# Attention weights read by VectorE and ScalarE from a lasting PSUM bank instead of an SBUF copy, in a graph attention layer

## The chip, the cores and the metric

The kernel runs on one core of one Trainium2 chip. The metric is the device time of one execution in microseconds. The engines are called PE (TensorE, whose weight loads are PEld), DVE (VectorE), ACT (ScalarE), POOL (GpSimd) and SP (SyncE, which here issues transfers).

## The reference

There are 12500 nodes with 256 features and 200000 edges sorted by their destination. A layer norm and a ReLU give h; then one graph attention layer with 8 heads of 32 features is computed, with gelu, a second layer norm, and residuals. Cut to what matters:

```python
h = relu(layernorm(x))
q, k, v = (h @ Wq + bq), (h @ Wk + bk), (h @ Wv + bv)      # each [n, 8, 32]
logits = einsum('ehd,ehd->eh', q[dst], k[src]) / sqrt(32)
seg_max = segment_max(logits, dst)
expv = exp(logits - seg_max[dst])
agg = segment_sum((expv / segment_sum(expv, dst)[dst])[:, :, None] * v[src], dst)
out = agg.reshape(n, 256) + (h @ Wskip + bskip)
y = h + gelu(out)
result = x + layernorm(y) * gamma + beta
```

## The kernel before, in words

First `project` normalizes x and writes a table of h and a table of k and v to HBM; beside it a plan is made of where each edge stands. This takes about the first 300 us. The rest is `walk_streams`.

The sorted edges are cut into 8 streams (S) of 25000 edges, which are walked side by side in 66 steps (NST). A step takes 384 slots (CH) of each stream, as 3 tiles (K) of 128 edges; the last step has 2 tiles, so that there are 197 tiles in all. Slot 0 of a step carries the running sums of the node that was open at the end of the step before. For tile j of step c:

- `gather` (L1047): 8 indirect transfers, issued by POOL, fetch the rows of k and v of 128 edges of each stream into one of 6 SBUF buffers `kv`. The gathers for step c + 2 are issued after the weighing that frees a buffer.
- `spread` (L1085, PE): matmuls with a one-hot matrix `to_e` spread the queries `qw` of the step's nodes over the edges, half of the streams at a time, into one of two PSUM buffers `ps_qe`. The queries themselves are projected in the walk (`turn_windows` L1023, `queries` L1036 and L1040, copied by ACT at L1026 and L1042); the one-hot matrices come from `hot_e` (L1062, L1064) and `hot_n` (L1073, L1075).
- `times` (L1094, DVE): product of queries and keys, a half at a time. `total` (L1101, DVE): sum over the 32 features, into L.
- `turn` (L1111, PE): transposes L into the PSUM bank `ps_x`, partitions 0 to 63 (8 streams by 8 heads), columns of tile j. For tile 0 ACT also copies the running maximum into column 0 (L1113).

Once per step, when all three tiles are turned:

- `maxima` (L1122, L1123, L1125, DVE): a scan forward (its result goes to the upper half of the bank), a scan backward, and the difference W. `exponent` (L1129, ACT).
- `turn_back` (L1137, PE): three transposes put the weights back, edges on partitions, into the first 192 columns of the bank; `weights` (L1145, ACT) copies them to SBUF as `w`, 128 x 192.
- `carried` (L1151, L1153, ACT): copies the carried denominators, and the weights of tiles 1 and 2 as the first 8 columns of `vw`. `weigh` (L1160, DVE): for each tile, `vw` is v times the weights; tile 0 has a second multiply for the denominators (L1165).
- `add_up` (L1184, PE) sums `vw` over the edges of each node in three groups of streams; ACT copies the sums (L1196) and the open node's row into the next step's tile 0 (L1202); SP stores them.

Beside that, in most steps from the tenth on, a `Pair` of blocks of finished nodes is normalized and stored (fetch, transposes L845, skip product L862, gelu L871, DVE statistics L874 to L880, root L884, factors L888 and L889, normal L894, shift L901 and L904, scale L908 and L910).

What sets the order: `keep` ties every instruction to the one before it on the same engine, so each engine runs the list in the order in which the loop from L1272 writes it. The loop at step c goes: halves of tile 2 of step c, `total`, `turn`; weighing of tile 2 of step c - 1; `maxima`; additions of step c - 1 around `exponent` and `turn_back`; `weights`; `carried`; tile 0 of step c + 1; weighing of tile 0; `hot_n`; `turn` of tile 0 of step c + 1; the pair's work and the projection for step c + 2; tile 1 of step c + 1, its `turn`; weighing of tile 1; additions of tiles 0 and 1; statistics of the pair. The framework adds the semaphore waits that the tiles' reads and writes call for.

In the kernel before, the bank is a tile that is taken anew for each step from a pool of one buffer (L1110), and its last readers are the scans and the copy L1145.

Of the kernel before, what the change touches and what calls it, by code (L numbers as in the profile page):

```python
# [28 lines left out]
F32 = mybir.dt.float32  # L29
# [10 lines left out]
P = 128  # L40
HEADS = 8
# [4 lines left out]
S = 8  # L46
K = 3
CH = K * P
# [705 lines left out]
def walk_streams(tc, N, HID, NST, KL, many, ident, idx, d0_row, slot_row, near, near_n, e_tab, pen_tab, h_tab,  # L754
# [6 lines left out]
    nc = tc.nc  # L761
# [3 lines left out]
    SH = S * HEADS  # L765
# [6 lines left out]
    def keep(ins):  # L772

        before = latest.get(ins.ins.engine)
        if before is not None:
            tc.add_manual_dep(ins.ins, before, mybir.DependencyInfo(
                mybir.DependencyClass.NoSync, mybir.DependencyReason.DATA), reason="kept order")
        latest[ins.ins.engine] = ins.ins.name
        return ins
# [168 lines left out]
    with ExitStack() as es:  # L948
# [8 lines left out]
        work = pool_of("work", 2)  # L957
# [3 lines left out]
        xt_ps = pool_of("xt_ps", 1, space=PSUM)  # L961
# [22 lines left out]
        def tiles_of(c):  # L984
            return KL if c == NST - 1 else K


        step = [dict() for _ in range(NST + 3)]

        def where(s):  # L990
# [115 lines left out]
        def turn(c, j):  # L1106

            g = step[c]
            if j == 0:
                g["xt"] = xt_ps.tile([P, 512], F32, name="ps_x")  # L1110
            keep(nc.tensor.transpose(g["xt"][:SH, j * P:(j + 1) * P], g["L"][:, j, :], ident))  # L1111
            if j == 0:
                keep(nc.scalar.copy(g["xt"][:SH, 0:1],  # L1113
                                    low0 if c == 0 else step[c - 1]["M"][:, CH - 1:]))

        def maxima(c):
            g = step[c]
            n = tiles_of(c) * P
            X, R, pen = g["xt"][:SH, :n], g["xt"][SH:, :n], g["pen"]
            M = g["M"] = work.tile([SH, CH], F32, name="M")[:, :n]  # L1120
            W = g["W"] = work.tile([SH, CH], F32, name="W", bufs=1)[:, :n]
            keep(nc.vector.tensor_tensor_scan(R, pen[:SH, :n], X, -BIG, op0=OP.add, op1=OP.max))  # L1122
            keep(nc.vector.tensor_tensor_scan(mirrored(M, 0, n), mirrored(pen[SH:, :], 1, n),  # L1123
                                              mirrored(R, 0, n), -BIG, op0=OP.add, op1=OP.max))
            keep(nc.vector.tensor_tensor(W, X, M, op=OP.subtract))  # L1125

        def exponent(c):
            W = step[c]["W"]
            keep(nc.scalar.activation(W, W, AF.Exp))  # L1129

        def turn_back(c):
            g = step[c]

            n = tiles_of(c)
            ps = g["xt"][:, :K * SH].rearrange("p (k n) -> p k n", k=K)
            for j in range(n):
                keep(nc.tensor.transpose(ps[:, j, :], g["W"][:, j * P:(j + 1) * P],  # L1137
                                         ident[:SH, :SH]))

        def weights(c):  # L1140
            g = step[c]
            n = tiles_of(c)
            ps = g["xt"][:, :K * SH].rearrange("p (k n) -> p k n", k=K)
            g["w"] = work.tile([P, K, SH], F32, name="w", bufs=1)
            keep(nc.scalar.copy(g["w"][:, :n, :], ps[:, :n, :]))  # L1145

        def carried(c):

            g = step[c]
            g["vw"] = [work.tile([P, S, SUMS], F32, name="vw", bufs=K) for _ in range(K)]  # L1150
            keep(nc.scalar.copy(wden[c % 2][0:1], g["kv"][0][0:1, :, HID - HEADS:HID]))  # L1151
            for j in range(1, tiles_of(c)):
                keep(nc.scalar.copy(g["vw"][j][:, :, :HEADS],  # L1153
                                    g["w"][:, j, :].rearrange("p (s h) -> p s h", s=S)))

        def weigh(c, j):
            g = step[c]
            t = g["vw"][j]
            wj = g["w"][:, j, :].rearrange("p (s h) -> p s h", s=S)
            keep(nc.vector.tensor_tensor(  # L1160
                t[:, :, HEADS:].rearrange("p s (h d) -> p s h d", h=HEADS),
                wj[:, :, :, None].to_broadcast([P, S, HEADS, D]),
                g["kv"][j][:, :, HID:].rearrange("p s (h d) -> p s h d", h=HEADS), op=OP.mult))
            if j == 0:
                keep(nc.vector.tensor_tensor(t[:, :, :HEADS], wj, wden[c % 2], op=OP.mult))  # L1165
# [106 lines left out]
        for c in range(NST - 1):  # L1272

            pair_next = None
            if c in due:
                pair_next = Pair(fin, due[c][0],
                                 lambda: hot_ps.tile([P, 2, KC, P], F32, name="ps_hot"),
                                 lambda: ag_ps.tile([P, 2 * HID], F32, name="ps_a").rearrange(
                                     "p (b d) -> p b d", b=2),
                                 keep)  # L1280
            if c + 3 < NST:
                windows(c + 3)
            for half in range(2):
                times(c, K - 1, half)
                spread(c + 1, 0, half)
            total(c, K - 1)
            turn(c, K - 1)
            if c:
                weigh(c - 1, K - 1)
                gather_next(c - 1, K - 1)  # L1290
            maxima(c)
            if before:
                before.factors()
            if c:
                add_up(c - 1, 0, range(K - 1, K))
                add_up_products(c - 1, 1)
            exponent(c)
            turn_back(c)
            if c:
                add_up_results(c - 1, 1)  # L1300
            weights(c)
            if c:
                add_up(c - 1, 2)
            carried(c)
            for half in range(2):
                times(c + 1, 0, half)
                spread(c + 1, 1, half)
            total(c + 1, 0)
            weigh(c, 0)
            gather_next(c, 0)  # L1310
            for j in range(K):
                hot_n(c, j)
            turn(c + 1, 0)
            if before:
                before.normal()
                before.shifted()
            if pair:
                pair.turn()
                pair.divisors()
                pair.divide()  # L1320
                pair.skip()
            if before:
                before.scale()
                before.store(0)
                before.store(1)
            if pair_next:
                pair_next.fetch()
            if c == NST - 2:
                for i in range(4):
                    last(i)  # L1330
            if c + 2 < NST:
                turn_windows(c + 2, 0)
                queries(c + 2, 0)
                hot_e(c + 2, 0)
            if pair:
                pair.add()
                table_of(AF.Gelu)
                pair.gelu()
            if c + 2 < NST:
                turn_windows(c + 2, 1)  # L1340
                queries(c + 2, 1)
            for half in range(2):
                times(c + 1, 1, half)
                if tiles_of(c + 1) == K:
                    spread(c + 1, K - 1, half)
            total(c + 1, 1)
            turn(c + 1, 1)
            weigh(c, 1)
            gather_next(c, 1)
            if c + 2 < NST:  # L1350
                for i in range(1, S // 2):
                    hot_e(c + 2, i)
            add_up(c, 0, range(K - 1))
            if c + 2 < NST:
                penalties(c + 2)
            if c + 3 < NST:
                prefetch(c + 3)
            if c == NST - 2:
                weigh(c, K - 1)
                add_up(c, 0, range(K - 1, K))  # L1360
                add_up(c, 1)
                if pair_next:
                    pair_next.turn()
                    pair_next.skip()
            if pair:
                table_of(AF.Sqrt)
                pair.stats()
                pair.root()
                table_of(AF.Exp)
            if c == NST - 2:  # L1370
                add_up(c, 2)
            before, pair = pair, pair_next
            if c > 1:
                step[c - 2] = None

        c = NST - 1
# [14 lines left out]
        if before:  # L1391
            before.factors()
        turn_back(c)
        weights(c)
        carried(c)
        weigh(c, 0)
        if pair:
# [53 lines left out]
        if extra:  # L1451
            with tc.If(many > 0):
                for m in extra:
                    p = Pair(fin, m, lambda: hot_ps.tile([P, 2, KC, P], F32, name="ps_hot"),
                             lambda: ag_ps.tile([P, 2 * HID], F32, name="ps_a").rearrange(
                                 "p (b d) -> p b d", b=2), lambda ins: ins)
# [349 lines left out]
```

## Time and profile before

| what | value |
| --- | --- |
| time, median of 7 runs | 3083.33 us (3051.05 to 3121.55) |
| the profiled execution's own time | 3099.2 us |
| its span, first to last instruction | 3097.4 us |
| granted TensorE clock, mean | 0.797 |
| the copy to SBUF (L1145) | 66 of 317 ns, 20.9 us in all |
| the copies into `vw` (L1153) | 131 of 238 ns, 25.2 us in all |
| the weighings (L1160) | 197 of 2286 ns, 450.2 us in all; 288.5 us idle before them |
| the transposes of L (L1111) | 197, 65.0 us in all |
| the scans forward (L1122) | 66 of 957 ns; 221.4 us idle before them |

A group's row gives the busy time, the mean of one instruction, and the idle time of its engine just before it with what ended that. In a timeline each row has its start, its duration, engine, line, operation, output and inputs, the count of merged instructions, and in brackets the idle time before it with what ended it. A matmul's end is modelled: its row says when it was issued, and the start of the instruction that waited for it says when it was done. An idle time put down to "remote" or "issue" has no releaser that the profile could name.

### The profile page before, as it was taken

Reading aid. Unit: us, or ns where it says so; the run is one execution under the profiler, and the core shown is the slowest. Engines: PE = TensorE matmul, PEld = TensorE weight load, DVE = VectorE, ACT = ScalarE, POOL = GpSimd, SP = SyncE. Lnnn points to the kernel's source line nnn. Section 1 sums busy time; section 2 is a strip of 40 time slices with the busy share of each in tenths; the row PEclk is TensorE's granted clock in tenths of the full one; section 3 lists DMA queues with packets and bytes.
Section 4 is the critical chain, followed back from the end, with each engine's and each line's share of the span. In section 5 each row is a group of like instructions: output and inputs, shape, how many; then the busy total and the mean of one; then the engine's idle time right before and its main releaser. Section 6 shows DMA issues by size and latency. Waiting matters only on the chain. (4 is left out here: it accounts for less than half of the span.)

```text
span 3097.4 us, 33801 instructions
## 1 busy us (share of the span) xinstructions
PE 2018.4 (65%) x10196; PEld 1161.5 (37%) x10196; DVE 1942.0 (63%) x2207; ACT 1111.0 (36%) x2583; POOL 1714.1 (55%) x1648
## 2 busy tenths in 40 slices
PE   7893666566566566577576667576666666665666
PEld 3441433333333343344343344343334333333333
DVE  8782665665566566566566566566566665666674
ACT  4330222222333344343344333343343343343343
POOL 2205476777566565556665566654656655655550
PEclk9996776877788788777787787777787878787786
DMA  8767466667576666666665676665666756765652
GB/s 277 259 221 233 129 193 190 197 186 216 171 212 193 196 185 187 188 195 198 212 200 171 189 211 194 199 187 165 207 193 192 210 173 183 207 194 175 194 157 80
DMA packets 285958, 597.79 MB, mean 193 GB/s; under 512 B 52295, under 2 KB 178452, under 8 KB 283584
## 3 DMA queue, kind: packets, MB, share of 16 engines
q0 software_dynamic: 128768, 423.23, 46.2%
q1 hardware_dynamic: 156466, 171.81, 17.4%
q8 instruction: 84, 1.38, 0.2%
q14 instruction: 110, 0.90, 0.1%
q10 hardware_dynamic: 530, 0.47, 0.1%
HBM read 512.83 MB, written 82.47 MB: 192 GB/s over the span
## 5 line engine op out<-in xcount | busy, mean ns | idle before, releaser
L1047 POOL DMA_INDIRECT kv<-kv_tab,idx x1576 | 1672.9, 1061 | 1085.9 <-issue 492.7
L1094 DVE TENSOR_TENSOR kv<-ps_qe,kv 128x1024 f32<-128x1024 f32 x394 | 468.2, 1219 | 402.3 <-remote 183.7
L1160 DVE TENSOR_TENSOR vw<-w,kv 128x2048 f32<-128x2048 f32 x197 | 450.2, 2286 | 288.5 <-ACT kv L1202 241.9
L1085 PE MATMUL ps_qe<-qw,to_e 64*128 64x256 f32 x3152 | 471.5, 440 | 19.0 <-issue 17.2
L1101 DVE TENSOR_REDUCE L<-kv 128x64 f32<-128x2048 f32 x197 | 450.4, 2286 | 6.7
L1085 PEld LDWEIGHTS ps_qe<-qw,to_e 64*128 64x128 f32 x3152 | 338.0, 218 | 169.1 <-issue 118.2
L1040 PE MATMUL ps_hot<-w_q,hwT 128*128 128x256 f32 x792 | 256.6, 470 | 121.0 <-issue 56.2
L1184 PE MATMUL ps_a<-vw,to_n 128*32 128x264 f32 (+1 forms) x2344 | 295.6, 494 | 43.6 <-DVE vw L1160 25.0
L1196 ACT COPY sums_w<-ps_a 128x264 f32<-128x264 f32 x130 | 49.3, 379 | 641.7 <-remote 412.6
L1064 ACT ACTIVATE to_e<-ps_hot,ones 128x384 f32<-128x384 f32 x264 | 145.6, 580 | 346.3 <-remote 256.0
L1184 PEld LDWEIGHTS ps_a<-vw,to_n 128*32 128x32 f32 (+1 forms) x2344 | 108.5, 141 | 396.6 <-issue 337.9
L1040 PEld LDWEIGHTS ps_hot<-w_q,hwT 128*128 128x128 f32 x792 | 170.0, 230 | 191.5 <-issue 77.3
L1062 PE MATMUL ps_hot<-et,near 48*128 48x384 bf16 x264 | 83.8, 357 | 239.3 <-ACT to_e L1064 148.6
L1073 PE MATMUL ps_hot<-near_n,et 48*128 48x384 bf16 x197 | 61.8, 357 | 272.5 <-ACT to_n L1075 161.6
L1137 PE MATMUL ps_x<-ident,W 64*128 64x64 f32 x197 | 31.0, 276 | 273.3 <-ACT W L1129 206.2
L248 PE MATMUL ps_kv<-w_kv,hT 128*128 128x512 f32 x392 | 188.7, 625 | 24.9 <-ACT hT L141 20.9
L1122 DVE TENSOR_TENSOR_SCAN ps_x<-pen,ps_x 64x384 f32<-64x384 f32 x66 | 63.1, 957 | 221.4 <-remote 137.8
L982 ACT ACT_TABLE_LOAD x138 | 177.1, 1283 | 2.4
L1042 ACT COPY qw<-ps_hot 128x256 f32<-128x256 f32 (+1 forms) x132 | 63.2, 479 | 280.4 <-PE ps_hot L1040 138.8
L1111 PEld LDWEIGHTS ps_x<-ident,L 128*64 128x64 f32 x197 | 22.5, 114 | 355.4 <-issue 282.1
L862 PE MATMUL ps_a<-w_s,hT 128*128 128x256 f32 x368 | 139.3, 544 | 16.3 <-ACT hT L848 11.4
L1202 ACT COPY kv<-ps_a 1x264 f32<-1x264 f32 x388 | 142.9, 368 | 6.3
(283 smaller groups left out, 2350.8 us busy)
## 6 DMA issues: line engine op xcount, KB each, us to landing
kv<-kv_tab,idx POOLq DMA_INDIRECT x1576
kv_tab<-kvo SPq DMA_DIRECT2D x14, 1536.0 KB
hw<-h_tab SPq DMA_DIRECT2D x264, 64.0 KB
table<-sums_w SPq DMA_DIRECT2D x264, 61.9 KB
pen<-pen_tab SPq DMA_DIRECT2D x66, 192.5 KB
sums<-table SPq DMA_DIRECT2D x92, 132.0 KB
x_f<-in_x_dram SPq DMA_DIRECT2D x92, 128.0 KB
h<-h_tab SPq DMA_DIRECT2D x92, 128.0 KB
```

Source lines behind the costliest of these rows:

```text
L248: ins = nc.tensor.matmul(ps_kv, hT[:, c, :], w_kv[:, c, :], start=c == 0, stop=c == KC - 1)
L862: self.keep(nc.tensor.matmul(self.ps[:, b, :], self.hT[:, b, c, :], w_s[:, c, :], start=False, stop=False, skip_group_check=True))
L982: keep(nc.scalar.activation(dummy[:, 1:2], dummy[:, 0:1], function))
L1040: keep(nc.tensor.matmul(ps[:, b, :], g["hwT"][:, b, k, :], w_q[:, k, :], start=False, stop=k == KC - 1, skip_group_check=True))
L1047: nc.gpsimd.indirect_dma_start(out=t[:, s, :], out_offset=None, in_=kv_tab[:, :], in_offset=bass.IndirectOffsetOnAxis(ap=idx[:, s, j, c:c ...
L1064: keep(nc.scalar.activation(step[c]["to_e"][:, i, :], ps[:, :CH], AF.Relu, scale=-1.0, bias=ones))
L1085: keep(nc.tensor.matmul(ps[:, b, a, :], g["to_e"][r, 2 * half + a, j * P:(j + 1) * P], g["qw"][r, (half + a) * half, :], start=True, stop= ...
L1094: keep(nc.vector.tensor_tensor(k, g["qe", half].rearrange("p b a d -> p a b d"), k, op=OP.mult))
L1101: keep(nc.vector.tensor_reduce(g["L"][:, j, :].rearrange("p (s h) -> p s h", s=S), g["kv"][j][:, :, :HID].rearrange("p s (h d) -> p s h d" ...
L1160: keep(nc.vector.tensor_tensor(t[:, :, HEADS:].rearrange("p s (h d) -> p s h d", h=HEADS), wj[:, :, :, None].to_broadcast([P, S, HEADS, D] ...
L1184: keep(nc.tensor.matmul(ps[at:at + w, :], g["to_n"][:, j, i * P + at:i * P + at + w], g["vw"][j][:, s, :], start=j == 0, stop=j == tiles_o ...
L1202: keep(nc.scalar.copy(step[c + 1]["kv"][0][0:1, s, HID - HEADS:], ps[at:at + 1, :]))
```

## The change

The bank becomes one tile for the whole walk, `turned`, with 512 columns. Columns 0 to 383 hold the transposed L of the step, as before. `turn_back` now writes the weights of tile 0 to columns 0 to 63, those of tile 1 to columns 384 to 447 and those of tile 2 to columns 448 to 511. `weights` and its copy L1145 are removed: `carried` and `weigh` read the weights in the bank. The order in which the loop writes the rest of a step is the same. (The queries are projected in the walk in both kernels.)

```diff
+        turned = xt_ps.tile([P, CH + 2 * SH], F32, name="ps_x")
...
         def turn(c, j):
             g = step[c]
+            keep(nc.tensor.transpose(turned[:SH, j * P:(j + 1) * P], g["L"][:, j, :], ident))
             if j == 0:
-                g["xt"] = xt_ps.tile([P, 512], F32, name="ps_x")
-            keep(nc.tensor.transpose(g["xt"][:SH, j * P:(j + 1) * P], g["L"][:, j, :], ident))
-            if j == 0:
-                keep(nc.scalar.copy(g["xt"][:SH, 0:1],
+                keep(nc.scalar.copy(turned[:SH, 0:1],
                                     low0 if c == 0 else step[c - 1]["M"][:, CH - 1:]))
...
-            X, R, pen = g["xt"][:SH, :n], g["xt"][SH:, :n], g["pen"]
+            X, R, pen = turned[:SH, :n], turned[SH:, :n], g["pen"]
...
+        def weight(j):
+            at = CH + (j - 1) * SH if j else 0
+            return turned[:, at:at + SH].rearrange("p (s h) -> p s h", s=S)
+
         def turn_back(c):
-            g = step[c]
-            n = tiles_of(c)
-            ps = g["xt"][:, :K * SH].rearrange("p (k n) -> p k n", k=K)
-            for j in range(n):
-                keep(nc.tensor.transpose(ps[:, j, :], g["W"][:, j * P:(j + 1) * P],
-                                         ident[:SH, :SH]))
-
-        def weights(c):
-            g = step[c]
-            n = tiles_of(c)
-            ps = g["xt"][:, :K * SH].rearrange("p (k n) -> p k n", k=K)
-            g["w"] = work.tile([P, K, SH], F32, name="w", bufs=1)
-            keep(nc.scalar.copy(g["w"][:, :n, :], ps[:, :n, :]))
+            for j in range(tiles_of(c)):
+                keep(nc.tensor.transpose(weight(j).rearrange("p s h -> p (s h)"),
+                                         step[c]["W"][:, j * P:(j + 1) * P], ident[:SH, :SH]))
...
             for j in range(1, tiles_of(c)):
-                keep(nc.scalar.copy(g["vw"][j][:, :, :HEADS],
-                                    g["w"][:, j, :].rearrange("p (s h) -> p s h", s=S)))
+                keep(nc.scalar.copy(g["vw"][j][:, :, :HEADS], weight(j)))
...
-            wj = g["w"][:, j, :].rearrange("p (s h) -> p s h", s=S)
+            wj = weight(j)
...
             turn_back(c)
             if c:
                 add_up_results(c - 1, 1)
-            weights(c)
```

More of the change, by code (lines that the diff above doesn't have):

```diff
@@ L1393, in walk_streams @@
         turn_back(c)
-        weights(c)
         carried(c)
```

## The prediction

> **What bounds the kernel now.** I read the page first (spans and engines), then the groups of the touched lines, then VectorE's waits, and last the timeline of one step of the walk, instruction by instruction.
>
> ```profile
> span 3097.4 us, 33801 instructions
> PE 2018.4 (65%) x10196; PEld 1161.5 (37%) x10196; DVE 1942.0 (63%) x2207; ACT 1111.0 (36%) x2583; POOL 1714.1 (55%) x1648
> ```
>
> No engine is full. The 66 steps are bound by the hand-written order: each engine runs its list, and a step lasts as long as the hand-overs between PE, DVE and ACT. Between the reductions L1101 of tile 2 in steps 1 and 63 a step takes 41.86 us on average. So a copy's busy time says little; what counts is who waits for it.
>
> ```profile
> L1153 ACT COPY vw<-w 128x64 f32<-128x64 f32 x131 | 25.2, 238 | 0.0
> L1145 ACT COPY w<-ps_x 128x192 f32<-128x192 f32 x66 | 20.9, 317 | 12.3 <-issue 5.2 <-PE ps_hot L1073 3.4 <-PE ps_x L1137 1.3
> ```
>
> The removed copy is 20.9 us of an engine that is 64% idle.
>
> ```profile
> DVE vw L1160 <- ACT kv L1202: 241.9, 48, 18.0
> DVE kv L1094 <- remote: 149.6, 42, 8.5
> ```
>
> The first weighing waits for the row copies L1202 (the sums carried over from the step before), not for the weights.
>
> ```profile
> 2070.95 0.76 ACT L1202 COPY kv<-ps_a 1x264 f32<-1x264 f32 x2
> 2071.74 2.29 DVE L1160 TENSOR_TENSOR vw<-w,kv 128x2048 f32<-128x2048 f32 x1 [4.31 <-ACT kv L1202]
> 2071.89 0.39 ACT L1153 COPY vw<-w 128x64 f32<-128x64 f32 x2
> ...
> 2073.33 0.42 PE L1111 MATMUL ps_x<-ident,L 128*64 128x128 f32 x1
> ...
> 2073.95 0.22 DVE L1165 TENSOR_TENSOR vw<-w,wden 128x64 f32<-128x64 f32 x1
> ...
> 2079.31 2.29 DVE L1101 TENSOR_REDUCE L<-kv 128x64 f32<-128x2048 f32 x1
> ...
> 2081.52 2.28 DVE L1160 TENSOR_TENSOR vw<-w,kv 128x2048 f32<-128x2048 f32 x1
> ...
> 2086.79 0.69 DVE L874 TENSOR_TENSOR sums<-sums,h 128x512 f32<-128x512 f32 x1 [2.99 <-ACT sums L871]
> ...
> 2088.19 0.30 DVE L880 BATCH_NORM_AGGREGATE mv<-st 128x2 f32<-128x6 f32 x2
> ...
> 2091.13 0.30 PE L1111 MATMUL ps_x<-ident,L 128*64 128x128 f32 x1
> ...
> 2093.53 1.23 DVE L1094 TENSOR_TENSOR kv<-ps_qe,kv 128x1024 f32<-128x1024 f32 x1 [5.03 <-DMA kv<-kv_tab,idx]
> 2098.03 1.23 DVE L1094 TENSOR_TENSOR kv<-ps_qe,kv 128x1024 f32<-128x1024 f32 x1 [3.28 <-remote]
> 2098.10 1.72 ACT L1064 ACTIVATE to_e<-ps_hot,ones 128x384 f32<-128x384 f32 x3 [8.21 <-remote]
> ...
> 2099.29 2.29 DVE L1101 TENSOR_REDUCE L<-kv 128x64 f32<-128x2048 f32 x1
> ...
> 2101.49 2.28 DVE L1160 TENSOR_TENSOR vw<-w,kv 128x2048 f32<-128x2048 f32 x1
> ...
> 2104.18 0.30 PE L1111 MATMUL ps_x<-ident,L 128*64 128x128 f32 x1
> ...
> 2104.52 0.96 DVE L1122 TENSOR_TENSOR_SCAN ps_x<-pen,ps_x 64x384 f32<-64x384 f32 x1 [0.74 <-PE ps_x L1111]
> ```
>
> See where the weighing of tile 1 stands (2081.52): ten microseconds before PE issues the transpose of the next step's tile 1 (2091.13). It fills a stretch in which VectorE would be idle. Then both VectorE (2098.03) and ScalarE (2098.10) start together, long after PE's modelled ends (2091.4): PE finished the spreading matmuls and the transpose late, at about 2098. I call that moment T2: the later of the modelled end of the transpose and, where the two halves of L1094 stand over 1.3 us apart, the start of the second half. Over steps 1 to 62 PE's lateness at T2 averages 2.9 us.
>
> **The change, part by part.** The columns in the shared bank are disjoint, but the built program of the changed kernel adds waits all the same. Followed by their counts: the weighing of tile 0 waits for both L1153 copies; the transpose of the next tile 0 waits for L1165; the weighings of tiles 1 and 2 wait for the transposes of the next step's tile 1 and the same step's tile 2, written just ahead of them. Before, VectorE took these weighings with no wait for PE.
>
> [...]
>
> *Removed copy.* 66 of 317 ns, ending at 2064.43 in the quoted step; ScalarE's next copy starts at 2070.67, held by PE. Worth 0; at most −20.9 us.
>
> *Weights read from PSUM.* Two L1094 (one operand in PSUM, 1024 each) take 2 x 1219 = 2438 ns, one L1160 (none in PSUM, 2048) 2286: the difference of 152 ns is one fixed start. Taken as 0; upper end 197 x 0.152 = 30 us; lower end 0, as the fixed part cannot be less than the one paid. The L1153 copies: L1145's short form from PSUM (128 wide) takes 238 ns like L1153's own: 0.
>
> *Tile 0.* Its weighing starts when the copies end, 2071.89 + 0.39 = 2072.28 instead of 2071.74: 0.54 later. L1165 then ends at 2074.17 + 0.54, and the transpose that stood at 2073.33 starts about 2074.8: 1.5 us later. Behind it on PE lie the shift matmuls, the skip product, both projections and the spreading, a chain with ScalarE that ends at T2. Where PE was already late it costs nothing: in the same way for steps 1 to 62 it is 0.92 us on average, 57 us.
>
> *Tile 1.* Its weighing moves from 2081.52 to T2, 16.5 us; in all 62 steps T2 is later than it (by 1.9 us at least, 11.2 on average). What is late next is VectorE: behind it are the statistics (0.69 + 0.75 + 0.30 with gaps: 1.7, in the 43 of 62 steps that hold a pair) and both halves of L1094. Before, the second half started at T2; now it starts at T2 + 2.3 + 1.7 + 1.2 (first half) = 5.2 later, without a pair 3.5. Where T2 was not late, the first half already overlapped; averages 5.1 and 3.3. 43 x 5.1 + 19 x 3.3 = 281 us. Eight gathers of L1047 are issued after this weighing; with them landing some 16 us later, cover is the median 23.8 us from the last issue to use. Gone, it would cost its shortfall. PE's add-up of tile 1 waits too, 0.8 us, ahead of spreading that waits for VectorE anyway. SP's transfers are not moved.
>
> *Tile 2.* Its weighing (2101.49) waits for the transpose, and the scan for the weighing. Before: scan 2.94 us after the reduction ended (2101.58). Now the spreading runs during the reduction, since VectorE is the late one; transpose 0.45, weighing 2.29: 2.74. Against each step's own scan the median is −0.9 us, 62 x −0.9 = −56: taken, as the middle step. Ends: if all PE lateness there vanishes, mean −2.9 (−177); if all stays, the weighing comes on top, +2.28 (+141).
>
> Sum: 0 + 0 + 57 + 281 − 56 = +282 us on the profiled execution's 3099.2 (span 3097.4), 3381; that execution stood 15.9 above the median, so **3365 us**. With the lower ends: −21 + 57 + 281 − 177 = +140, 3223; with the upper: 30 + 57 + 281 + 141 = +509, 3592.
>
> **The rivals.**
> 1. *Not slower.* VectorE's delay gives PE rest and its lateness vanishes at both places: T2 62 x −2.9 = −181 and the scan −177: −21 + 281 + 57 − 181 − 177 = −41, 3042. It decides once the lateness falls by 338 of these 358 us. For it: the clock is granted at 0.78 to 0.80 through the walk. Against: step 23 took 57.4 us, and the halves of the next step's L1094 still stood 5.2 apart.
> 2. *Worse.* PE gets slower as it idles more. PE is busy 1731.7 us from 300 to 3000; were the granted clock 0.75 instead of 0.797 and all of that on the path, 6%: 108 us more, 3473, or with the upper ends 3700. For: the clock is below full now, with PE idle 35% of the time. Against: the same idle gaps are there now. [...]
> 3. *The new waits do not bind* because they are met early, or only addresses count: then only tile 0 costs, +57: 3140. Against: T2 is later in every step.
>
> **How the numbers follow.** Forecast 0.82; rival 1 0.04; rival 2 beyond the range 0.09; rival 3 0.05. The range 3210 to 3530 holds the forecast's ends short of the last, and leaves out the rivals. About 1% (31 us) is what a measurement of this kernel can tell from no change: faster 0.02, same 0.03 (rival 1 splits), slower 0.95.
>
> **What would show it.** Right: L1145 gone; the weighing's group gaining idle time released by PE's transposes of L, some 11 us per step on tile 1; the transposes' wait released by L1165; the reductions of tile 2 some 46 us apart instead of 41.9; the weighing's mean still near 2286 ns. Wrong: a weighing of tile 1 still ahead of the transpose, a mean above 2.4 us, a granted clock much off 0.80, or gathers that VectorE waits for.

## The result, and the profile after

The changed kernel takes 3365.62 us (median of 18 runs, 3357.10 to 3374.93) against 3084.30 us for the kernel before (46 runs, 3046.99 to 3125.02): a ratio of 1.0945, 95% interval 1.0923 to 1.0968, or +281 us. The forecast was 3365 us. The total came out as forecast; the places where the time went did not, and most of what follows is about that.

In the changed kernel the lines have moved a little: the weighing is L1153 (L1160 before), the copies of the weights into their rows L1147 (L1153), the copies of the sums L1189 and L1195 (L1196 and L1202), the products of VectorE L1096 (L1094), the reduction L1103 (L1101). The lines of the page and of its groups that answer to those shown of before:

```profile
span 3366.3 us, 33800 instructions
PE 2274.3 (68%) x10196; PEld 1255.0 (37%) x10196; DVE 1944.5 (58%) x2207; ACT 1097.8 (33%) x2517; POOL 1551.5 (46%) x1648
...
L1153 DVE TENSOR_TENSOR vw<-ps_x,kv 128x2048 f32<-128x2048 f32 x197 | 451.3, 2291 | 1187.2 <-ACT vw L1147 595.0
```

VectorE and ScalarE do the same work as before. The copy L1145 is gone (66 instructions fewer on ScalarE). A weighing that reads PSUM takes 2291 ns instead of 2286. But the idle time just before the weighings is 1187.2 us. The waits of the engines name who ends it (total, times, longest):

```profile
DVE vw L1153 <- ACT vw L1147: 595.0, 64, 11.5
DVE vw L1153 <- PE ps_x L1111: 532.1, 67, 12.5
```

The first line is tile 0, which waits for the copies of the other tiles' weights; the second is tile 1, which waits for the transpose of the next step. Now one step in order of time (start, duration, engine, line; the brackets hold the idle time ahead and who ended it):

```profile
2199.13 0.96 DVE L1122 TENSOR_TENSOR_SCAN ps_x<-pen,ps_x 64x384 f32<-64x384 f32 x1
...
2200.19 2.91 PE L1177 MATMUL ps_hot<-vw,to_n 128*64 128x264 f32 x12
...
2200.33 0.38 ACT L1189 COPY sums_w<-ps_a 128x264 f32<-128x264 f32 x1 [7.22 <-PE ps_a L1177]
...
2203.03 0.58 PE L1138 MATMUL ps_x<-ident,W 64*128 64x64 f32 x3
...
2212.66 0.38 ACT L1189 COPY sums_w<-ps_hot 128x264 f32<-128x264 f32 x1 [10.09 <-remote]
...
2215.04 0.33 ACT L1147 COPY vw<-ps_x 128x64 f32<-128x64 f32 x2
...
2215.40 2.29 DVE L1153 TENSOR_TENSOR vw<-ps_x,kv 128x2048 f32<-128x2048 f32 x1 [8.78 <-ACT vw L1147]
...
2217.88 0.42 PE L1111 MATMUL ps_x<-ident,L 128*64 128x128 f32 x1 [1.50 <-DVE vw L1158]
...
2234.32 0.30 PE L1111 MATMUL ps_x<-ident,L 128*64 128x128 f32 x1
...
2234.66 2.29 DVE L1153 TENSOR_TENSOR vw<-ps_x,kv 128x2048 f32<-128x2048 f32 x1 [8.51 <-PE ps_x L1111]
2236.86 0.68 DVE L874 TENSOR_TENSOR sums<-sums,h 128x512 f32<-128x512 f32 x1
...
2238.55 2.36 DVE L1096 TENSOR_TENSOR kv<-ps_qe,kv 128x1024 f32<-128x1024 f32 x2
...
2243.61 2.29 DVE L1153 TENSOR_TENSOR vw<-ps_x,kv 128x2048 f32<-128x2048 f32 x1 [0.39 <-issue]
2245.94 0.96 DVE L1122 TENSOR_TENSOR_SCAN ps_x<-pen,ps_x 64x384 f32<-64x384 f32 x1
```

Every wait that the forecast named is there: the transpose that waits for L1158 (1.50), the weighing of tile 1 behind the transpose (8.51), then the statistics and both halves of L1096, now back to back ("x2"), then the weighing of tile 2 ahead of the scan. What the forecast did not have is the wait of 10.09 us at 2212.66: PE issued the products of ps_hot at 2200.19, their modelled end is 2203.10, and ScalarE's copy gets them 9.6 us later. Everything down to the first weighing at 2215.40 stands behind this copy.

I cut each step into stretches by the instructions' times and averaged them over steps 1 to 62, as in the forecast. The last column counts the instructions of ScalarE and VectorE between 400 and 2950 us that wait for PE and start over 1 us after the modelled end of what they wait for (and after their own engine's last instruction), with the sum of these delays; where two engines wait for one delay it counts twice. In the changed kernels the first weighings are counted as well, since they read the bank, though what they wait for are ScalarE's copies.

| kernel | reduction of tile 2 to scan | scan to first weighing | to tile 1's first product | to tile 2's second product | step | late, sum us |
|---|---|---|---|---|---|---|
| before | 7.88 | 11.84 | 4.79 | 16.09 | 41.86 | 206, 1036 |
| changed | 5.27 | 16.74 | 5.05 | 17.78 | 46.08 | 118, 1079 |
| difference | −2.61 | +4.90 | +0.26 | +1.69 | +4.22 | |

(The rest of a step, second product to reduction, is 1.25 us in all.) 62 x 4.22 = 262 us of the 281 lie in these steps. The two sums look alike, but PE's lateness has become smaller. With every moment counted once it is about 790 us in the kernel before; of the 1079 us of the changed kernel 516 are first weighings, which wait for ScalarE's copies behind ps_hot, and without them some 560 us are left. And it has moved: before, it is spread over the copies of the sums (480 us), the products L1094 (155), to_e (193) and the scan (139); in the changed kernel it is nearly all at one place, the copies of ps_hot, 10.0 us in each of 55 steps (550 us), with the first weighings behind them (516). It is PE that the copy waits for, and no transfer: the copy at 2212.66 waits for one semaphore alone, PE's, and the trace has a raise of it at 2212.64. In the kernel before nine in ten of the late waits end within 0.15 us of such a raise.

### The profile page after: what moved, and what is told of

Its sections match the earlier page's. It is cut to its first block, busy times and chain, and to the rows that moved or that the text cites. A ratio compares the mean times of both kernels' runs of the same rounds, so it can differ in the third digit from the quotient of the medians.

```text
span 3366.3 us, 33800 instructions
## 1 busy us (share of the span) xinstructions
PE 2274.3 (68%) x10196; PEld 1255.0 (37%) x10196; DVE 1944.5 (58%) x2207; ACT 1097.8 (33%) x2517; POOL 1551.5 (46%) x1648
## 3 DMA queue, kind: packets, MB, share of 16 engines
q0 software_dynamic: 128768, 423.23, 43.0%
## 4 chain that ended last, share of the span: by engine, by line
PE 29%; issue 23%; another core or an unknown queue 16%; ACT 14%; DVE 13%; DMA 3%; POOL 1%; SPq 1%; DVEq 0%; ACTq 0%; POOLq 0%
PE ps_qe L1087 6%; PE ps_hot L1042 5%; ACT kv L1195 4%; PE ps_kv L248 4%; DVE vw L1153 4%; DVE L L1103 3%; PE ps_hot L904 3%; DVE kv L1096 2%; PE ps_a L1177 2%; ACT sums_w L1189 2%; PE ps_a L862 2%; ACT L982 2%; ACT hwT L1028 1%; PE ps_hot L1177 1%
## 5 line engine op out<-in xcount | busy, mean ns | idle before, releaser
L1049 POOL DMA_INDIRECT kv<-kv_tab,idx x1576 | 1510.0, 958 | 1523.4 <-DVE vw L1153 523.1
L1153 DVE TENSOR_TENSOR vw<-ps_x,kv 128x2048 f32<-128x2048 f32 x197 | 451.3, 2291 | 1187.2 <-ACT vw L1147 595.0
L1087 PE MATMUL ps_qe<-qw,to_e 64*128 64x256 f32 x3152 | 612.9, 472 | 387.1 <-issue 274.6
L1087 PEld LDWEIGHTS ps_qe<-qw,to_e 64*128 64x128 f32 x3152 | 401.4, 228 | 568.2 <-issue 530.8
L1096 DVE TENSOR_TENSOR kv<-ps_qe,kv 128x1024 f32<-128x1024 f32 x394 | 463.2, 1216 | 72.3 <-remote 34.8
L1103 DVE TENSOR_REDUCE L<-kv 128x64 f32<-128x2048 f32 x197 | 450.4, 2286 | 6.7
L1177 PE MATMUL ps_a<-vw,to_n 128*32 128x264 f32 (+1 forms) x2344 | 280.5, 467 | 194.2 <-DVE vw L1153 171.0
L1189 ACT COPY sums_w<-ps_hot 128x264 f32<-128x264 f32 x68 | 25.7, 378 | 658.8 <-remote 526.0
L1189 ACT COPY sums_w<-ps_a 128x264 f32<-128x264 f32 x130 | 49.2, 378 | 512.1 <-PE ps_a L1177 267.2
L1177 PE MATMUL ps_hot<-vw,to_n 128*64 128x264 f32 x808 | 185.7, 626 | 1.7 <-DVE o L910 1.7
L1075 PE MATMUL ps_hot<-near_n,et 48*128 48x384 bf16 x197 | 92.3, 475 | 137.0 <-ACT to_n L1077 111.4
L862 PE MATMUL ps_a<-w_s,hT 128*128 128x256 f32 x368 | 153.7, 588 | 7.6 <-ACT hT L848 1.2
L1111 PE MATMUL ps_x<-ident,L 128*64 128x128 f32 x197 | 70.3, 357 | 118.2 <-DVE vw L1158 89.1
L1111 PEld LDWEIGHTS ps_x<-ident,L 128*64 128x64 f32 x197 | 23.3, 119 | 339.5 <-DVE vw L1158 261.4
L1195 ACT COPY kv<-ps_a 1x264 f32<-1x264 f32 x388 | 142.9, 368 | 6.3
```

The lines of the kernel that those rows point to most:

```text
L862: self.keep(nc.tensor.matmul(self.ps[:, b, :], self.hT[:, b, c, :], w_s[:, c, :], start=False, stop=False, skip_group_check=True))
L1049: nc.gpsimd.indirect_dma_start(out=t[:, s, :], out_offset=None, in_=kv_tab[:, :], in_offset=bass.IndirectOffsetOnAxis(ap=idx[:, s, j, c:c ...
L1087: keep(nc.tensor.matmul(ps[:, b, a, :], g["to_e"][r, 2 * half + a, j * P:(j + 1) * P], g["qw"][r, (half + a) * half, :], start=True, stop= ...
L1096: keep(nc.vector.tensor_tensor(k, g["qe", half].rearrange("p b a d -> p a b d"), k, op=OP.mult))
L1103: keep(nc.vector.tensor_reduce(g["L"][:, j, :].rearrange("p (s h) -> p s h", s=S), g["kv"][j][:, :, :HID].rearrange("p s (h d) -> p s h d" ...
L1153: keep(nc.vector.tensor_tensor(t[:, :, HEADS:].rearrange("p s (h d) -> p s h d", h=HEADS), wj[:, :, :, None].to_broadcast([P, S, HEADS, D] ...
```

## The experiments

They ran on other chips than the result: there the kernel before takes 3179 to 3197 us. So all comparisons are ratios to the kernel before on the same chip. Two theories stood at the start. The forecast's theory: each new wait costs by itself, as worked out. The gate theory: the new order makes PE's pauses longer, PE's granted clock halves behind them (in the step above from 1.00 at 2208 to 2212 to 0.52 at 2212 to 2214; the mean granted clock fell from 0.797 to 0.745), and the work behind the scan runs at half clock, hence the 4.90 us.

**Which weighing pays.** Four kernels keep the lasting bank, copy the weights to SBUF again, and let no weighing, or only that of one tile (with the copy of its weights into its row), read PSUM:

```diff
+        def read(c, j):
+            if j in FROM_PSUM:
+                return weight(j)
+            return step[c]["w"][:, j, :].rearrange("p (s h) -> p s h", s=S)
...
-            wj = weight(j)
+            wj = read(c, j)
```

FROM_PSUM is empty, (0,), (1,) and (2,). What was expected:

> The lasting bank and its new columns stay, but the weights are copied to SBUF again (two copies a step) and every weighing reads the copy. Both theories put the whole price on the weighings' reads of PSUM, so both expect the time before, about 3084 us (within 1%). If the lasting bank by itself costs (a transpose that waits for readers of another step's columns), it is above 3115 us.

> As the control, but the weighing of tile 0 reads PSUM. The forecast's theory (each wait costs by itself, as worked out): +57 us, 3141 us. The gate theory (most of the price comes when PE's pauses get long enough to halve its granted clock ahead of the work after the scan): this wait makes no new pause near the scan, so less than that, 3084 to 3120 us.

> As the control, but the weighing of tile 1, and the copy of its weights into its row, read PSUM. The forecast's theory: +281 us, 3365 us, nearly the whole change, with the stretch from the scan to the first weighing as before (11.8 us). The gate theory: VectorE's own delay is worth what the trace of the changed kernel shows of it, 1.7 us a step or 105 us, 3190 us; what comes on top shows as a longer stretch from the scan to the first weighing, at most 4.9 us a step (3493 us).

> As the control, but the weighing of tile 2 reads PSUM. The forecast's theory: between 0 and the upper end of its term for tile 2, 62 x 2.28 = 141 us, as VectorE is not held by tile 1 here: 3084 to 3225 us. The gate theory: PE's products of tile 2 start later behind a pause of some 2.4 us, one pause and not two, so little of the 4.9 us a step after the scan: 3084 to 3150 us. If the three tiles add up to about 282 us, the prices are separate; if they add up to much less or more, they act together.

| kernel | us | ratio, 95% | to scan | to first weighing | to tile 1 | to second product | step | late, sum us |
|---|---|---|---|---|---|---|---|---|
| none | 3189.39 | 1.0005 (0.9963–1.0048) | 9.43 | 12.20 | 4.72 | 15.57 | 43.18 | 205, 1176 |
| tile 0 | 3211.21 | 1.0041 (0.9996–1.0085) | 10.05 | 12.19 | 5.36 | 14.77 | 43.62 | |
| tile 1 | 3335.30 | 1.0415 (1.0297–1.0534) | 4.40 | 10.91 | 7.87 | 20.94 | 45.37 | 160, 603 |
| tile 2 | 3305.96 | 1.0333 (1.0255–1.0410) | 9.64 | 12.66 | 4.45 | 17.16 | 45.17 | 180, 887 |

The columns are those of the first table. With none the time is that of the kernel before, as both theories had it. With tile 0 alone the forecast's 57 us lie outside the interval and the gate theory's range (0 to 36 us) holds it. With tile 1 alone the price is far below the forecast's and near the 105 us of the gate theory, but without the longer stretch behind the scan that would go with its theory. With tile 2 alone it lies in the forecast's range and above that of the gate theory (66 us).

The bank by itself costs nothing (1.0005). Of 3196 us the three reads cost 13, 133 and 106 us (the ratios less one, times before), 252 together, or 7.9%, against the 9.45% of the change; with these intervals they can be separate prices that add up, though a difference of some 50 us would not show. But they are not the forecast's: it had 57, 281 and −56. Tile 1 alone shows why. Its delay of VectorE is there in full, even above the forecast's 5.5: the stretches from the first weighing to the second product grow by 28.81 − 20.29 = 8.5 us. But 5.0 us come back at the scan and 1.3 behind it, as PE's results are no longer late at the scan, and less late at the copies of the sums behind it.

**Which way round the waits stand.**

```diff
-            turn(c, K - 1)
             if c:
                 weigh(c - 1, K - 1)
+            turn(c, K - 1)
+            if c:
                 gather_next(c - 1, K - 1)
...
-            turn(c + 1, 1)
             weigh(c, 1)
+            turn(c + 1, 1)
             gather_next(c, 1)
```

> The changed kernel with two pairs of lines exchanged: the weighing of tile 1 is written ahead of the transpose of the next step's tile 1, that of tile 2 ahead of the same step's transpose of tile 2. Each engine's own order stays; the transposes now wait for the weighings instead of the other way round. The forecast's theory: tile 1's 5.5 us a step go; tile 0's +57 us stays and the weighing of tile 2 stands ahead of the scan as it did: 3084 + 57 to + 141 = 3141 to 3282 us, a ratio to before of 1.018 to 1.064. The gate theory: PE's pause ahead of the tile-1 products goes as well, so at most the same, but the transpose of tile 2 still waits and the pause ahead of the scan stays: 1.02 to 1.06. Both expect well under the changed kernel's 1.0945; if it stays there, the direction of the waits is not what costs.

3348.11 us, ratio 1.0548 (1.0493 to 1.0603), inside both expectations: with the same instructions in the same order on each engine, the direction of two waits is worth some 0.04 of the 0.0945. The stretch from the scan to the first weighing is 12.63 us. The stretch from tile 1's first to tile 2's second product is longer, though, 21.67 us against 17.78, and results of PE are late in it again (the products L1096, to_e and the projections, some 620 us). So with the gathers it is not enough to turn the waits round. This doesn't part the theories, and it doesn't reach the kernel before.

**The gate theory.** Matmuls that nobody reads fill PE's pauses ahead of the scan, or, as a control, the busy stretch behind it:

```diff
+        def fill(c, n):
+            for _ in range(n):
+                keep(nc.tensor.matmul(step[c]["bank"][:, SUMS:2 * HID], w_q[:, 0, :P],
+                                      w_q[:, 0, :2 * HID - SUMS], start=False, stop=False,
+                                      skip_group_check=True))
...
             if c:
+                fill(c - 1, 6)
                 add_up(c - 1, 0, range(K - 1, K))
...
             add_up(c, 0, range(K - 1))
+            fill(c, 6)
```

> The changed kernel with 12 more matmuls a step on PE whose results nobody reads (128x128 weights, 248 columns, f32, into the free columns of a bank that PE holds): 6 where PE waits for the weighing of tile 1 and VectorE's products, 6 where it waits for the weighing of tile 2. The forecast's theory: PE's lateness is no matter of its clock, so 62 x 12 x 0.25 us of work into waits gains nothing: a ratio to before of 1.09 to 1.15. The gate theory: the granted clock behind these pauses stays at full instead of half, the stretch from the scan to the first weighing shrinks from 16.7 towards 11.8 us, the mean granted clock rises above 0.78: a ratio of 0.99 to 1.05.

> The kernel before with the same 12 matmuls at the same two places. The forecast's theory: no gain, 1.00 to 1.06 of before. The gate theory: the clock at the scan and behind it is halved in a third to a half of the steps here too, and PE is 2.85 us late at the scan: up to 62 x 2.85 = 177 us are to be had, a ratio of 0.94 to 1.00.

> Control for the filling: the changed kernel with the 12 matmuls right behind the products that follow the scan, where the gate theory has PE as the engine that sets the end, at half its clock. The gate theory: each costs its own time there, 0.25 to 0.5 us, 3 to 6 us a step, 186 to 372 us: a ratio to before of 1.155 to 1.215. The forecast's theory, in which PE has slack in this stretch (it names none of its terms there): 1.09 to 1.12.

| kernel | us | ratio, 95% | granted clock | scan to first weighing | step |
|---|---|---|---|---|---|
| changed, pauses filled | 3501.08 | 1.1026 (1.0969–1.1084) | 0.826 | 17.27 | 48.07 |
| before, pauses filled | 3293.40 | 1.0386 (1.0323–1.0449) | 0.838 | 13.05 | 44.80 |
| changed, busy stretch filled | 3492.17 | 1.1001 (1.0939–1.1064) | 0.826 | 18.60 | 47.83 |

(Each of the matmuls is two instructions in the trace, 11744 of PE against 10196, so the filling is 24 a step, 12 at each place.) All three ratios lie in the ranges of the forecast's theory and outside those of the gate theory. The filling raised the mean clock, and in the 3 us behind the scan of the first kernel it rose from 0.54 to 0.90 (means of steps 1 to 62); the time did not follow. Over the whole stretch to the first weighing the clock stayed at 0.70, and the lines below show why. The ratios alone do not exclude that the filling gained something which its own work took away again: it added 0.039 to the kernel before and 0.008 to the changed one.

One step of the first kernel shows more. First instructions in order of time, then stretches of 3 us with the busy time and number of instructions of PE, PEld, DVE, ACT and POOL, the granted clock, the DMA share and the GB/s:

```profile
2263.21 0.65 PE L1178 MATMUL ps_a<-vw,to_n 128*32 128x264 f32 x8
...
2263.80 1.56 PE L1178 MATMUL ps_hot<-vw,to_n 128*64 128x264 f32 x12
...
2274.38 0.38 ACT L1190 COPY sums_w<-ps_a 128x264 f32<-128x264 f32 x1 [16.80 <-remote]
```

```profile
2263.00:2266.00 3.00, 2.35 (x22) 0.93 (x20) 2.85 (x7) 0.00 (x0) 2.09 (x4) 1.00 0.72 213
2266.00:2269.00 3.00, 0.00 (x0) 0.00 (x0) 2.97 (x3) 0.00 (x0) 2.39 (x3) 1.00 0.72 210
2269.00:2272.00 3.00, 0.00 (x0) 0.00 (x0) 1.63 (x1) 0.00 (x0) 2.31 (x3) 0.65 0.73 195
```

The products of ps_a are issued at 2263.21 with the clock at 1.00, and their result is 10.5 us late. The clock falls only at 2270, after PE has stood still: in this step the low clock follows the lateness and isn't its cause. With this the gate theory falls as the reason for the 4.90 us, and a kernel further below confirms it: the changed one without lookups runs at the same low clock (0.55 in the 3 us behind the scan, 0.72 in the stretch) and its stretch is 7.81 us. The last two columns gave the next theory. Here are stretches of the kernel before, at the moment that the prediction calls T2 (2098):

```profile
2090.00:2092.00 2.00, 1.86 (x15) 1.04 (x12) 0.00 (x0) 0.00 (x0) 1.70 (x2) 1.00 1.02 292
2092.00:2094.00 2.00, 0.00 (x0) 0.00 (x0) 0.47 (x1) 0.00 (x0) 1.39 (x3) 1.00 1.06 355
2094.00:2096.00 2.00, 0.00 (x0) 0.00 (x0) 0.75 (x1) 0.00 (x0) 1.63 (x2) 1.00 1.05 298
2096.00:2098.00 2.00, 0.00 (x0) 0.00 (x0) 0.00 (x0) 0.00 (x0) 0.00 (x0) 0.68 0.91 296
2098.00:2100.00 2.00, 1.27 (x9) 0.40 (x12) 1.93 (x2) 1.79 (x4) 0.00 (x0) 0.50 0.05 20
```

and of the changed kernel, at the copy of ps_hot (2212.66):

```profile
2208.00:2212.00 4.00, 0.82 (x3) 0.37 (x2) 0.00 (x0) 0.00 (x0) 1.65 (x2) 1.00 0.70 206
2212.00:2214.00 2.00, 1.74 (x6) 0.77 (x6) 0.00 (x0) 1.29 (x5) 0.00 (x0) 0.52 0.06 20
```

In both, PE comes free when the transfers end: the DMA share falls from 0.91 to 0.05 and from 0.70 to 0.06 in the very slice in which the engines go on. The transfers that end there are POOL's gathers of K and V rows, 8 a tile. In the changed kernel the copy of ps_hot starts within 1 us of the end of a bunch of gathers in 52 of the 60 steps from 2 to 61. Of the late waits of the first table, 205 of 206 and 118 of 118 are for results whose modelled end lies inside such a bunch. That says less than it seems, since the bunches cover 80% of the walk in the kernel before and 69% in the changed one, and most results inside them come in time (some 1400 of 1600 in the kernel before; of some 460 outside none is late). So it takes an experiment.

**The gathers.** In both kernels the lookups are left out: SP fetches fixed rows of the same size, so the outputs are other ones.

```diff
             for s in range(S):
-                nc.gpsimd.indirect_dma_start(
-                    out=t[:, s, :], out_offset=None, in_=kv_tab[:, :],
-                    in_offset=bass.IndirectOffsetOnAxis(ap=idx[:, s, j, c:c + 1], axis=0))
+                keep(nc.sync.dma_start(t[:, s, :], kv_tab[s * P:(s + 1) * P, :]))
```

> The kernel before with the gathers of K and V left out: SP fetches as many rows of the same 2 KB, but fixed ones, into the same tiles at the same place in the order, so the output is another. In the trace of before PE's results come later than their modelled ends in 173 episodes of the walk, 910 us in all, and 172 of them begin while POOL's gathers move data; in the changed kernel it is 141 and 1056 us, 133 of them. The theory of the gathers (PE is held up while POOL's gathers move data): with POOL's gathers gone the lateness mostly goes, below 300 us, and the time falls to 2500 to 2900 us. The theory of the traffic (any transfers of that size hold PE up): lateness 700 us or more, 2950 to 3200 us. The gate theory: PE's pauses are those of the order, so lateness and clock stay, 3000 to 3200 us.

> The changed kernel with the same replacement. The theory of the gathers: what the change costs was mostly PE's lateness behind two bunches of gathers close together, so it lies within 0 to 4% of the kernel of the other run with the direct fetches, and the stretch from the scan to the first weighing is under 12 us instead of 16.7. The theory of the traffic and the gate theory: 7 to 12% above it, the stretch at 15 us or more.

A third kernel keeps POOL as the issuer (`nc.gpsimd.dma_start` with the same operands), and a fourth is the changed kernel with SP's fetches and the weighings written ahead of the transposes:

> The kernel before with the gathers left out, as in the run with SP's direct fetches, but POOL issues the same fixed rows of 2 KB, 8 transfers where it issued 8 gathers. If it is the looking up of rows (indirect transfers) that holds PE's results up, the time is that of SP's fetches, 2400 to 2600 us, with next to no late episodes. If it is anything that POOL issues, PE's lateness stays at 600 us or more in 100 episodes or more, and the time lies between 2800 and 3250 us.

> The changed kernel with SP's direct fetches (gathers left out) and with both weighings written ahead of the transposes. With nothing to hold PE's results up, the changed kernel took 232 us more than the kernel before in the same form (2693.7 against 2461.1). The theory that this is the price of the two weighings' waits for the transposes: with the waits the other way round it goes but for tile 0's and for the transpose of tile 2 behind its weighing (up to 2.3 us a step, 141 us): 2460 to 2610 us, the stretch of tile 1 back from 17.0 to about 13.5 us. If it is the bank itself, or the transposes that wait, it stays near 2690 us.

| kernel | us | ratio, 95% | to scan | to first weighing | to tile 1 | to second product | step | late, sum us |
|---|---|---|---|---|---|---|---|---|
| before, SP | 2461.14 | 0.7702 (0.7667–0.7737) | 4.40 | 7.53 | 5.73 | 13.45 | 32.38 | 39, 84 |
| changed, SP | 2693.68 | 0.8421 (0.8388–0.8455) | 5.18 | 7.81 | 4.74 | 17.01 | 35.99 | 14, 16 |
| before, POOL | 2082.07 | 0.6532 (0.6487–0.6576) | 4.40 | 7.29 | 4.06 | 9.68 | 26.68 | 0, 0 |
| changed, SP, weighings ahead | 2465.65 | 0.7739 (0.7686–0.7792) | 4.90 | 7.40 | 5.58 | 13.25 | 32.39 | 31, 66 |

The page of the third:

```profile
span 2083.6 us, 33797 instructions
PE 1672.2 (80%) x10196; PEld 995.9 (48%) x10196; DVE 1918.2 (92%) x2207; ACT 1103.4 (53%) x2583; POOL 894.6 (43%) x1648
...
q0 software_dynamic: 128768, 423.23, 59.7%
```

The queue of POOL moved as many packets and bytes as in the two kernels with gathers (128768 packets, 423.23 MB), at more GB/s (287 of all queues on average against 193 and 178), and no result of PE came late. So it is not the traffic and not POOL's queue; it is the lookup of rows, or what comes with it (rows spread over the table, where the plain transfers fetch the same 1024 rows each time). Two times lay outside what was expected: 2461 us is a little below the 2500 to 2900 of the theory of the gathers, and 2082 us far below the 2400 to 2600 of the theory of the lookups, which took no account of the time that SP's fetches cost by themselves (2461 us against POOL's 2082). The 910 and 1056 us of the first expectation come from the times at which PE's semaphore was raised; of these raises the trace of before holds only 1833 of 2187, that of SP's fetches 2186, so I counted again by the engines that wait, as in the tables.

For the change itself the second and the fourth row matter. The theory of the gathers had expected 0 to 4% for the second. It is 232.5 us or 9.45% of 2461, as much as with the gathers, so in this it fails: the change costs with hardly a late result (16 us). In the other point it holds: the stretch from the scan to the first weighing is 7.81 us against 7.53, so the 4.90 us of the first table go with the gathers. The waits of VectorE in that kernel, whose lines stand two higher (L1151 is the weighing), say where:

```profile
DVE vw L1151 <- PE ps_x L1109: 526.3, 128, 10.1
...
DVE vw L1151 <- ACT vw L1145: 36.4, 32, 5.7
```

128 waits of a weighing for a transpose, 526.3 us; and the stretch that grew is that of tile 1 (13.45 to 17.01). With the weighings ahead of the transposes 228 of the 232.5 us are gone, as the theory of the waits expected. A limit: the first and the fourth of these kernels are held by SP's fetches too (the chain that ended last puts 36% and 37% on DMA, and VectorE waits for kv, the sums and the windows), so a rest of the price may be hidden there. The changed kernel with POOL's plain transfers, which would be free of that, was not run.

## Why the prediction was right in sum and wrong in its parts

- *Removed copy and reads from PSUM*: taken as 0 and 0. Right for the reads: a weighing takes 5 ns more, 1 us in all; the upper end of 30 us is far off. No run takes the copy alone away. Nothing speaks against 0: without gathers the kernel that has no copy and the weighings ahead is at 2465.65 against 2461.14 us.
- *Which waits bind*: right, all of them, though the columns are disjoint: the weighings of the changed kernel wait for the copies L1147 (595.0 us, 64 times) and for the transposes of L (532.1 us, 67 times), the weight loads of the transposes for L1158 (261.4 us, 65 times). So this program does not wait by addresses alone: the third rival's 3140 us is out.
- *Tile 0*, +57: too much, 13 us alone (−1 to 27).
- *Tile 1*, +281: the step that failed. "Before, the second half started at T2; now it starts at T2 + 2.3 + 1.7 + 1.2" holds T2 fixed. T2 was late while the gathers issued behind the weighings of tiles 0 and 1 were moving, until 2098. With the weighing at T2 the latter start later as well, and T2 itself is no longer late: in the changed kernel the products L1096 and to_e are never over 1 us late. The stretch grew by 1.69 us a step instead of 5.1 and 3.3; alone, tile 1 costs 133 us.
- *Tile 2*, −56: alone it costs +106 us, within the ends given (−177 to +141); but alone VectorE is not the late one, which is the case of the upper end, so this is no test of the −56. In the whole change the lower end came nearest: −2.61 us a step from the reduction to the scan against −0.9 forecast and −2.9 as the end.
- *What no term had*: +4.90 us a step from the scan to the first weighing. The 8 gathers behind the weighing of tile 1 (2237.22 on) now run straight into those behind tile 2, so one bunch of 16 covers the scan and what hangs on it, and the results of ps_hot wait for its end (in 52 of 60 steps their copy starts within 1 us of it). The forecast looked at these gathers only for whether they land in time.
- *Rival 1* was right on its mechanism: PE's lateness at T2 and at the scan went. But much of it came back at another place, which the rival did not ask. *Rival 2* was right on the clock (0.745 against its 0.75), and its price did not show: with the clock lifted to 0.826 by the filling the time did not fall.
- *The signs*: steps 46.08 us apart, the transpose's wait for L1158 and 2291 ns are signs of right. The wait of tile 1 is 8.6 us a step and not 11. And the clock at 0.745 is one of its signs of wrong, "much off 0.80".

So the total of 281 against 282 is in part luck: −2.61 + 4.90 + 0.26 + 1.69 = 4.24 us a step stands against a forecast of 4.5 made of other parts. What isn't luck is that the order itself has a price of this size: with next to nothing late (84 and 16 us) it is 232.5 us, and turning two waits round takes 228 of them away. With the gathers the same exchange takes away only 0.04 of the 0.0945. How the gathers' delay and the order add up to the same 9.45% with and without gathers was not settled.

## What to carry to other kernels

When a buffer moves into a PSUM bank that another engine writes, list what stands ahead of each new reader in the program in that bank; writing the reader ahead of the writer took the ratio from 1.0945 to 1.0548 here without moving an instruction on any engine. Don't hold another engine's lateness fixed while you move work past it: first find what it waits for, and ask where that goes. Here a result came 10.5 us late from a PE that stood idle and had been granted 1.00 of its clock at the issue, and in the kernel before with plain transfers from POOL none was over 1 us late: replace the transfers that run at such a time by plain ones of the same size before you build a theory on the clock.

## What the runs showed of the hardware that was not expected

- While POOL's lookups move rows, PE's results can come late: 206 waits, 1036 us, in the kernel before, none with plain transfers of the same bytes from POOL, which take the time from 3192 to 2082 us. What the lookups hold up, and whether looking up rows in another way avoids it, was not tried.
- In the walk of the kernel before (400 to 3000 us) the granted clock was 1.00 or 0.50, in records of 3.41 us or a multiple of it, and went with PE's busy time in slices of that length (by modelled ends): all 83 full-clock slices under 40% busy were followed by one at half clock, 2 of 304 above 60% were; all 111 rises came after a slice over 90% busy, but 52 of 163 such slices at half clock brought none.
- A VectorE operand in PSUM instead of SBUF cost 5 ns on 2286 (the 64 weights of a row, each read 32 times; the other operand in SBUF).
